# Choosing the unit blocks of a feed-forward layer: a multiply on GpSimd with a mask spread by DMA, in place of a third product on TensorE

## The chip, the cores and the metric

The kernel runs on one core of one Trainium2 chip. The metric is device time in microseconds of one execution. The time before is 1347.35 us, the median of three runs (1347.07 to 1347.78). Five engines work side by side, each with its own queue of instructions that it takes strictly in order: TensorE (PE in the profile; its weight loads are PEld), VectorE (DVE), ScalarE (ACT), GpSimd (POOL), and SyncE (SP), which here only issues DMAs.

## The reference

Two layers of a transformer block over x of shape 8 x 512 x 256. Layer 0 is an attention with 16 heads plus a mixture of 32 experts, layer 1 a small gelu layer plus a feed-forward layer whose units are chosen in blocks. Only the last one matters here:

```python
BLOCK, NBLK = 64, 16                  # 16 blocks of 64 hidden units
TOPK = NBLK // 4                      # a token keeps 4 of the 16 blocks
prob = softmax(xf @ router_w.T + router_b)
...
y = einsum('nib,dib->nd', where(mask[:, :, None], h, 0.0), w2b) + b2
```

Here h is relu(xf @ w1.T + b1), 1024 units to a token, and mask marks the 4 blocks with the largest prob. So a token's hidden units count only in the blocks that it chose.

## The kernel before

**An order made by a planner.** The kernel does not issue its work line by line. It first builds a list of operations (`op`, L156), each with an engine, a key, the function that issues its instructions, the operations it needs, a due time (`prio`), and the buffers that it takes (`acq`) and gives back (`rel`). `emit` (L206) then walks through a model of the five engines and picks, again and again, the operation that can start first; it issues the instructions in that order. The model's costs stand in the table `TIMES` (L52), the due times are shifted by the table `SHIFT` (L99), and `choose` (L295) prefers, on TensorE, an operation that keeps the tile layout of the one before (`SAME`, `OTHER`, L293). The layouts are F (the whole array), R (two halves of its rows), C (two halves of its columns), E and Q (quarters), G. Whatever the planner decides becomes the fixed order of every engine's queue; on the chip, semaphores only make an engine wait.

**The attention stage.** For 32 pairs of (batch, group of four heads), `produce` (L872) projects q, k, v, normalizes and transposes q and k; `attend` (L1133) then makes scores, an exponential, a division on GpSimd (`divide`, L1181), a transposition (`turn`, L1186; L419), its copies to SBUF into a buffer `prT` (L1199, L1201; two such buffers exist), and the product with v (`values`, L1222). The experts run in between. This stage fills the span up to about 1000 us.

**The second layer.** `second` (L1688) is called once for each of the eight batches b. With the lines that matter, in the order in which a batch goes through them:

- `s.root` (L1714, POOL): one over the root of the variance, 128x4. It comes after `s.eps` on DVE. `s.b2` (L1723, POOL, four to a batch) adds the output bias to the residual.
- `s.xn` (L1718, DVE, four) normalizes, `s.xT` (L1729, PE) transposes; the copies follow (L1735, L1737).
- `s.lg` (L1746, PE) makes the router's logits, `s.lgt` (L1768, PE) turns them; DVE and ACT make the softmax and mark the four largest (L1777 to L1792, `s.rep`).
- `s.off` (L1797, DVE) writes 1.0 for a block that is *not* chosen. `s.mt` (L1803, PE) turns these 128x128 tiles with four bf16 products, `s.mo` (L1810, ACT) copies them to SBUF as `offT`, a tile of 128 x 512 in which row k tells of block k.
- `s.narrow` and `s.gelu` (L1817, L1825): the small layer beside it.
- `s.hid` (L1844, PE), four times, two tiles of 128 units x 512 tokens each: two fp32 products for each tile (L1849), and a **third product** (L1853) of a constant table `blkm` with `offT`. `blkm` has -2^100 where a unit belongs to block k, so the sum becomes hugely negative for all units of the blocks that were left out.
- `s.relu` (L1865, ACT): relu with the bias. What was left out comes out as zero.
- `s.start` (L1888, PE) begins the output in PSUM with the small layer's part, `s.down` (L1896, PE), four to a batch, adds the product with w2; `s.out` (L1904, DVE) adds the residual, and a DMA on SP's queue writes 128 KB to the output (L1909).

The batches overlap: while batch b is in its `s.hid`, the four `s.down` of batch b-1 are put in between, and the front part of batch b+1. The tables `blkm` and the two buffers for `s.off` are made once by `c_masks` (L1514, key `w.masks`, POOL) in one of the five 4 KB buffers `ew`.

Of the kernel before, what the change touches and what calls it, by code (L numbers as in the profile page):

```python
# [11 lines left out]
ALU = mybir.AluOpType  # L12
# [33 lines left out]
class Op:  # L46
# [5 lines left out]
    "warm": (4137, 4117), "n.turn": (165, 317), "p1.qk": (2004, 1984), "p1.v": (891, 1041),  # L52
    "p.turn": (259, 412), "p2.qk.a": (1775, 1937), "p2.qk.b": (1730, 1932), "g.turn": (118, 282),
    "a.score2": (803, 976), "a.score0": (335, 497), "gt.turn": (328, 308), "a.score3": (1100, 1238),
    "p2.v.a": (897, 1041), "p2.v.b": (900, 1042), "a.turn2": (425, 586), "a.turn0": (140, 291),
    "a.score1": (541, 711), "a.turn3": (516, 662), "a.turn1": (289, 417), "a.y": (2305, 2374),
    "c.logits": (1854, 1924), "eb.turn": (608, 679), "c.turn": (605, 656), "c.merge": (1865, 1933),
    "c.mturn": (368, 439), "o.proj.a": (3468, 3674), "o.proj.b": (3500, 3628), "e.hidden": (1854, 1924),
    "e.turn": (493, 655), "e.down": (1865, 1934), "w.t1.t": (446, 600), "w.t3.t": (495, 565),
    "w.t4.t": (164, 328), "w.t2.t": (586, 650), "w.fold.t": (1035, 1106), "j.go": (1075, 1145),  # L60
    "s.xT0.t": (447, 600), "s.xT1.t": (437, 600), "s.lg": (574, 644), "s.lgt": (165, 327),
    "s.narrow": (949, 1084), "s.mt": (224, 387), "s.hid": (3873, 4029), "s.start": (532, 626),
    "s.down": (3471, 3617), "n.stat": (329, 408), "n.aggr": (76, 150), "gw.uk": (335, 417),
    "n.eps": (64, 156), "n.xv": (350, 410), "gw.sum": (328, 410), "n.out0": (200, 278),
    "gw.prod": (598, 686), "gw.max": (70, 308), "gw.red": (598, 676), "gw.inv": (85, 164),
    "gw.mul": (71, 150), "qw": (37, 116), "om1": (82, 157), "p.sum": (599, 682), "p.mean": (74, 168),
    "om3": (86, 172), "p.g": (75, 156), "p.scale": (663, 693), "p.gs": (72, 156), "p.k1": (261, 343),
    "p.k0": (261, 342), "om4": (184, 164), "om5": (195, 175), "g.least": (108, 196), "g.relu": (78, 168),
    "g.s0": (69, 166), "g.s1": (159, 252), "g.s2": (82, 176), "g.s3": (91, 176), "g.s4": (81, 174),
    "g.s5": (90, 175), "g.s6": (162, 192), "g.s7": (84, 174), "see": (15, 60), "g.s8": (90, 166),  # L70
    "g.s9": (89, 175), "g.s10": (91, 175), "g.s11": (84, 174), "g.s12": (74, 174), "g.s13": (104, 174),
    "g.out0": (333, 416), "a.most2": (475, 662), "a.most0": (208, 392), "a.inv": (79, 160),
    "a.most3": (606, 791), "a.out02": (467, 551), "gt.out": (121, 206), "a.out00": (198, 281),
    "a.most1": (340, 526), "a.out03": (601, 685), "n.shift": (70, 155), "a.out01": (326, 412),
    "c.max": (584, 676), "c.inv": (176, 156), "c.prob": (425, 494), "c.max8": (592, 676),
    "c.rest": (673, 678), "eb.out": (331, 416), "c.sel": (615, 682), "c.out": (604, 688),
    "c.mout": (364, 425), "c.min": (334, 416), "o.add": (337, 416), "e.hout": (599, 689),
    "e.bias": (603, 680), "e.out": (332, 418), "w.t1.o": (601, 682), "w.t3.o": (469, 449), "w.wide": (0, 0),
    "w.t4.o": (1207, 1187), "w.fold.o": (201, 284), "j.add": (600, 682), "s.tiles": (0, 0),
    "s.stat": (320, 408), "s.aggr": (84, 166), "s.eps": (100, 170), "s.xn": (394, 599),  # L80
    "s.xT0.o": (605, 691), "s.lgb": (267, 351), "s.most": (174, 219), "s.sub": (139, 224),
    "s.sum": (137, 220), "s.inv": (88, 178), "s.prob": (179, 226), "s.max8": (78, 159), "s.top": (150, 178),
    "s.rep": (143, 165), "s.off": (215, 195), "s.out": (340, 425), "gw.sq": (361, 418),
    "n.out1": (155, 270), "p.qk": (477, 586), "p.sq": (531, 633), "om2": (219, 199), "p.v": (259, 372),
    "p.q0": (252, 364), "p.q1": (255, 367), "biasrows": (733, 798), "g.exp": (117, 216),
    "g.out1": (257, 364), "a.exp2": (608, 809), "a.exp0": (400, 596), "a.out12": (363, 474),
    "a.exp3": (716, 917), "a.out10": (156, 266), "a.exp1": (501, 702), "a.out13": (467, 586),
    "n.xa": (497, 601), "a.out11": (330, 372), "a.yout": (473, 585), "c.bias": (585, 687),
    "c.exp": (723, 918), "e.gelu0": (536, 630), "e.gelu1": (521, 624), "w.t2.o": (473, 607),
    "s.xT1.o": (605, 585), "s.exp": (276, 256), "s.gelu": (403, 383), "s.mo": (471, 586),  # L90
    "s.relu": (707, 687), "masks": (855, 891), "rows": (2373, 2353), "slopes": (613, 593),
    "n.root1": (516, 556), "clear": (544, 524), "gw.root": (987, 1010), "p.root": (1622, 1643),
    "zeros": (251, 311), "g.off": (236, 216), "g.part": (305, 389), "g.rest": (409, 434), "begun": (0, 0),
    "a.div2": (569, 585), "a.div0": (347, 371), "a.div3": (667, 691), "n.root4": (985, 1013),
    "a.div1": (450, 478), "w.masks": (3007, 3024), "w.small": (166, 187), "w.fill": (537, 572),
    "s.root": (1037, 1017), "s.b2": (746, 768),
# [3 lines left out]
    "c.bias": -3.29, "s.max8": 3.57, "p.q0": 2.42, "w.t4.o": -5.8, "s.eps": -9.92, "c.max8": 2.15,  # L100
    "p2.v.a": -3.63, "s.mt": 5.88, "a.exp3": -4.3, "w.t4.t": -0.13, "o.proj.b": 0.15, "s.lgt": -7.35,
    "c.exp": 2.7, "p.sum": -5.14, "c.mout": 0.03, "s.b2": 7.43, "s.xT1.o": -4.3, "s.lgb": -4.56,
    "a.out10": 0.14, "a.exp1": -0.68, "a.yout": -3.47, "s.exp": -10.95, "a.most0": 0.35, "g.s3": 3.95,
    "s.narrow": -4.78, "s.root": -4.04, "s.sum": 1.37, "g.s6": 2.17, "s.most": -2.85, "s.stat": -0.87,
    "s.prob": -1.71, "p.sq": -1.43, "w.fold.o": 2.03, "p.gs": -2.82, "c.turn": 1.44, "g.s12": 1.31,
    "s.top": -6.26, "g.s10": -1.46, "g.s2": 3.5, "eb.turn": -2.98, "w.t1.o": -3.61, "om1": -7.04,
    "biasrows": 4.93, "a.div0": 6.33, "gw.root": -2.34, "gw.inv": -3.63, "s.gelu": -0.89, "a.out13": 1.66,
    "masks": -48.39, "s.start": 5.05, "g.s9": -2.47, "w.small": -3.28, "w.fill": 15.3, "s.xT0.o": -1.94,
    "n.root1": 1.13, "n.root4": 3.27, "g.least": 2.04, "e.out": -0.02, "gt.out": -2.41, "c.logits": -7.82,
    "s.off": 4.99, "clear": 3.53, "g.relu": 0.52, "warm": -21.2, "g.s0": -1.94, "a.turn3": 0.39,  # L110
    "a.score3": -1.07, "g.s4": -1.71, "s.inv": -4.39, "qw": -14.97, "g.s5": 5.68, "g.exp": -1.07,
    "om2": -5.05, "a.turn2": 1.14, "e.gelu0": 5.01, "p.q1": -5.55, "j.go": -3.38, "c.min": 8.72,
    "a.out00": 2.71, "e.turn": -1.46, "a.y": 1.34, "s.hid": -2.92, "s.sub": -9.5, "w.fold.t": -8.73,
    "p.qk": -0.3, "a.inv": -1.61, "gw.uk": -5.57, "c.out": 2.42, "n.shift": 7.81, "a.turn1": -0.19,
    "p.g": -3.58, "e.hidden": 0.67, "c.merge": 4.93, "a.div2": -2.99, "p.mean": -0.88, "slopes": -2.76,
    "a.div1": -2.14, "a.out12": 0.32, "g.out1": 0.43, "a.out02": 2.95, "e.gelu1": -0.41, "s.relu": -1.14,
    "o.add": -4.81, "n.turn": -1.67, "w.t2.o": 1.33, "a.most3": -3.64, "g.s11": -2.41, "s.out": 7.6,
    "n.xa": 7.52, "om4": 10.76, "w.t3.o": 1.73, "g.turn": -1.73, "g.s1": 5.26, "c.prob": 2.06,
    "c.rest": 3.9, "c.mturn": 9.1, "begun": 1.87, "gw.prod": 1.93, "rows": -0.26, "n.eps": -2.59,
    "j.add": -4.89, "e.hout": 1.27, "s.mo": -1.28, "n.aggr": -8.37, "c.inv": 5.78, "s.tiles": -5.37,  # L120
    "a.score0": -1.86, "s.xT1.t": -3.79, "gw.red": -4.57, "p2.v.b": -1.01, "e.bias": -0.22, "p.v": -5.67,
    "g.part": 0.41, "g.out0": 0.1, "p.k0": -1.07, "c.max": 5.04, "om5": 2.2, "s.xT0.t": -5.16,
    "o.proj.a": 1.19, "s.lg": -9.54, "a.out03": -2.66, "g.rest": 5.2, "eb.out": -6.2, "gt.turn": 6.11,
    "see": -4.13, "gw.sum": 2.3, "s.aggr": -12.41, "a.exp2": 1.42, "g.s7": 5.88, "p1.v": 5.24,
    "s.xn": -3.43, "w.t3.t": -3.47, "gw.max": -3.1, "g.off": 6, "p.scale": 3.47, "w.t1.t": -2.48,
    "w.t2.t": 0.97, "p2.qk.b": 0.14, "s.down": 7.43, "a.out01": -0.8, "a.exp0": 1.45, "g.s13": 1.57,
# [1836 lines left out]
```

## Time and profile before

| what | value |
|---|---|
| median of the runs | 1347.35 us |
| the profiled execution's own time | 1349.12 us |
| its span | 1347.4 us |
| TensorE busy in the span | 1302.8 us |
| the same, 50 to 1000 us | 925.13 of 950 us |
| the same, 1000 to 1100 us | 95.63 of 100 us |
| the same, 1100 to 1347.4 us | 243.69 of 247.4 us |
| GpSimd busy, 1100 to 1347.4 us | 22.18 of 247.4 us |
| third products (L1853) | 64, first at 1048.6 us, last at 1325.2 us |

The profile is of one execution, whose own time is 1.7 us above its span. Busy time of TensorE is modelled: matmuls are pipelined, a matmul's listed duration reaches into the next one's, so what one costs is read from the distance between starts. In a timeline row the columns are: start, busy time of the merged row, engine, line, operation, out<-in, tile of the array, shape, count, and in brackets the idle time before it and who ended it.

### The profile page before, as it was taken

To read this page: it belongs to the slowest core of one execution; us is meant where nothing else is said; L and a number is where in the kernel's file an instruction comes from. 1 tells how busy PE (TensorE), PEld (TensorE's weight loads), DVE (VectorE), ACT (ScalarE), POOL (GpSimd) and SP (SyncE) were. 2 spreads that over 40 slices of the span, in tenths; PEclk is the share of its full clock that TensorE was granted. 3 is DMA by queue.
4 is the path that set the end of the run, shared out by engine and by line. 5 is a ranking of instruction groups with operands and counts; after the bars stand their busy time and mean duration, and the time that the engine had idled before them with its cause. 6 is when DMAs were issued, how large, how long until landed. Compare 5 with 4: busy or idle time off the path is not lost.

```text
span 1347.4 us, 32371 instructions
## 1 busy us (share of the span) xinstructions
PE 1302.8 (97%) x11831; PEld 829.9 (62%) x11840; DVE 901.1 (67%) x3712; ACT 820.6 (61%) x2268; POOL 621.4 (46%) x1115
## 2 busy tenths in 40 slices
PE   7899999999999999999999999999999999999998
PEld 4555666556655665665565656656665576666666
DVE  5889987787777778867877677778869433232300
ACT  3687876676677757766866766777757522222221
POOL 4666644656456555645565455555545311111100
PEclk8899999999999999999999999999999999999999
DMA  7002001431143032322323231142120000000000
GB/s 225 5 1 80 2 2 63 143 127 67 64 145 118 12 127 84 117 78 81 125 69 126 80 132 64 64 147 67 56 71 17 1 13 13 16 17 16 16 20 20
DMA packets 74575, 90.65 MB, mean 67 GB/s; under 512 B 5272, under 2 KB 57744, under 8 KB 74416
## 3 DMA queue, kind: packets, MB, share of 16 engines
q1 hardware_dynamic: 73856, 88.16, 19.5%
q8 instruction: 93, 1.52, 0.5%
q14 instruction: 66, 0.54, 0.1%
q10 hardware_dynamic: 560, 0.43, 0.1%
HBM read 84.11 MB, written 4.19 MB: 66 GB/s over the span
## 4 chain that ended last, share of the span: by engine, by line
PE 69%; DVE 19%; ACT 5%; POOL 4%; issue 2%; DMA 1%; SPq 0%; DVEq 0%; ACTq 0%; POOLq 0%
PE w L440 25%; PE w L1896 8%; PE w L1849 8%; PE w L1155 7%; PE w L1227 6%; PE w L419 5%; DVE pr L1164 5%; DVE prT L1201 3%; POOL rs L964 2%; DVE ss L957 2%; DVE tm L967 2%; PE w L1151 2%; PE w L1337 1%; DVE k L991 1%; ACT pr L1172 1%
## 5 line engine op out<-in xcount | busy, mean ns | idle before, releaser
L1182 POOL TENSOR_SCALAR pr<-pr,rinv 128x384 f32<-128x384 f32 (+3 forms) x512 | 284.6, 573 | 241.9 <-DVE rinv L1179 177.4
L1172 ACT ACTIVATE pr<-pr,nm 128x384 f32<-128x384 f32 (+3 forms) x512 | 285.6, 563 | 47.6 <-DVE nm L1164 38.8
L964 POOL TENSOR_TENSOR rs<-ss,nhalf 128x8 f32<-128x8 f32 x128 | 213.6, 1671 | 152.4 <-DVE ss L960 139.6
L1164 DVE CUSTOM_DVE_ANT_0 pr<-w,later 128x384 f32<-128x384 f32 (+3 forms) x512 | 241.3, 485 | 49.3 <-PE w L1155 47.0
L440 PE MATMUL w<-wqk_sb,xnT 64*128 64x512 f32 x992 | 243.4, 605 | 0.8 <-DVE ms L817 0.2
L1155 PE MATMUL w<-k,q 64*128 64x128 f32 (+3 forms) x1024 | 189.3, 442 | 0.0
L1227 PE MATMUL w<-prT,v 128*64 128x512 f32 (+3 forms) x1024 | 154.1, 443 | 9.4 <-DVE prT L1201 5.0
L1199 ACT COPY prT<-w 128x512 f32<-128x512 f32 (+3 forms) x256 | 106.5, 430 | 84.0 <-PE w L419 83.4
L419 PEld LDWEIGHTS w<-ident,pr 64*128 64x128 f32 x2560 | 115.5, 139 | 64.7 <-issue 38.7
L440 PEld LDWEIGHTS w<-wqk_sb,xnT 64*128 64x128 f32 x992 | 93.3, 188 | 69.1 <-issue 61.1
L1227 PEld LDWEIGHTS w<-prT,v 128*64 128x64 f32 x1024 | 72.1, 138 | 101.5 <-issue 62.6
L1201 DVE COPY prT<-w 128x512 f32<-128x512 f32 (+3 forms) x256 | 122.8, 485 | 11.2 <-PE w L419 9.7
L440 PE MATMUL w<-wvg_sb,xnT 64*128 64x260 f32 x992 | 126.5, 388 | 0.0
L419 PE MATMUL w<-ident,pr 64*128 64x64 f32 x2560 | 120.9, 223 | 5.2 <-DVE k L991 1.9
L1849 PE MATMUL w<-xT,mT 128*128 128x512 f32 x256 | 120.6, 593 | 0.5
L440 PE MATMUL w<-wp_sb,yT 64*128 64x256 f32 x1024 | 117.1, 379 | 1.0 <-DVE seen L451 0.7
L1904 DVE TENSOR_TENSOR ot<-w,x 128x256 f32<-128x256 f32 x32 | 13.5, 423 | 149.1 <-PE w L1896 149.1
L440 PEld LDWEIGHTS w<-wp_sb,yT 64*128 64x128 f32 x1024 | 99.4, 187 | 17.0 <-issue 3.4
L1155 PEld LDWEIGHTS w<-k,q 64*128 64x128 f32 x1024 | 89.3, 189 | 21.4 <-issue 17.5
L938 ACT COPY tm<-w 128x512 f32<-128x512 f32 x128 | 72.9, 588 | 47.8 <-PE w L440 29.2
L957 DVE TENSOR_REDUCE ss<-sq 128x8 f32<-128x512 f32 x128 | 87.2, 681 | 22.1 <-ACT sq L942 22.1
L967 DVE TENSOR_TENSOR tm<-tm,rs 128x512 f32<-128x512 f32 x128 | 90.7, 710 | 13.2 <-POOL rs L964 12.7
(210 smaller groups left out, 2025.0 us busy)
## 6 DMA issues: line engine op xcount, KB each, us to landing
ew<-in_L_ffn_w_dram SPq DMA_DIRECT2D x128, 512.0 KB
x<-in_L_attn_x_dram SPq DMA_DIRECT2D x15, 512.0 KB
out_dram<-ot SPq DMA_DIRECT2D x32, 128.0 KB
raw<-in_L_ffn_w_dram SPq DMA_DIRECT2D x4, 512.0 KB
wqk_sb<-in_L_attn_Wk_dram SPq DMA_DIRECT2D x4, 256.0 KB
wqk_sb<-in_L_attn_Wq_dram SPq DMA_DIRECT2D x4, 256.0 KB
wp_sb<-in_L_attn_Wproj_dram SPq DMA_DIRECT2D x1, 1024.0 KB
b2g<-in_L_ffn_w_dram SPq DMA_DIRECT2D x32, 32.0 KB
```

The source lines that it names most:

```text
L419: nc.tensor.transpose(out, blk, ident[rows, rows])
L440: x = nc.tensor.matmul(m.outs[i], lhs(i, k, rows), rhs(k, rows), start=(part == k == 0), stop=(part == 1 and k == n - 1))
L957: nc.vector.tensor_reduce(s.ss[t], s.sq[t], AX.X, ALU.add)
L964: nc.gpsimd.tensor_tensor(s.rs[t], s.ss[t], nhalf[:, : 2 * HG], ALU.pow)
L967: nc.vector.tensor_mul(s.tm[t], s.tm[t], s.rs[t].unsqueeze(2).to_broadcast([P, 2 * HG, D]),)
L1155: nc.tensor.matmul(m.sc[h][:, :w], s.qT[k, q, n0:w], s.kT[k, q, :w], start=False, stop=True)
L1164: nc.vector.tensor_tensor_reduce(m.p[:, h, :], m.sc[h][:, :w], later[:, T - w :], -1.0, BIG, ALU.add, ALU.min, m.nm[:, h : h + 1],)
L1172: nc.scalar.activation(m.p[:, h, :], m.p[:, h, :], AF.Exp, bias=m.nm[:, h : h + 1], scale=-1.0, accum_out=m.sums[:, h : h + 1],)
L1182: nc.gpsimd.tensor_scalar(m.p[:, h, :], m.p[:, h, :], m.rinv[:, h : h + 1], 1.0, ALU.mult, ALU.mult)
L1201: nc.vector.tensor_copy(dst, src)
L1227: nc.tensor.matmul(pp.yp[h * D : (h + 1) * D, j * P :], s.v[j][:, hh * D : (hh + 1) * D], pp.tri[:, :, h, j : j + 4 * (NT - 1 - j) + 1 : 4 ...
L1849: nc.tensor.matmul(m.ph[i], w1T[:, dc, k * P : (k + 1) * P], s.xT[:, dc, :], start=(dc == 0), stop=False,)
```

## The change

The mask is now applied after the relu, by a multiply. `s.off` writes 1.0 for a *chosen* block, in fp32, into the place of the probabilities. `s.mt` turns 128 x 16 to 16 x 128 four times in fp32. `s.mo` copies 16 rows. Then a DMA sends these 16 rows of 512 tokens (bf16) to a scratch tile in DRAM, and two DMAs read it back so that each of the 128 partitions gets the row of its own block, for all eight tiles: a mask of 128 x 8 x 512 bf16, 1 MB. It lies in one of the two buffers `prT`, which the attention has used. Third products, `blkm` and `c_masks` go. GpSimd multiplies each rectified tile by its mask in place (`s.keep`, 128x512, 64 in all), and `s.start` waits in the plan for the multiplies instead of the relus. `s.hid` no longer needs the mask.

The rest is the planner's: all numbers of `TIMES` and `SHIFT` are others, and so are `SAME` and `OTHER`. The order of the whole kernel is made anew from them, in the attention stage too.

```diff
-    "c.bias": -3.29, "s.max8": 3.57, "p.q0": 2.42, "w.t4.o": -5.8, "s.eps": -9.92, "c.max8": 2.15,
+    "c.bias": -4.03, "s.max8": -0.29, "p.q0": -5.16, "w.t4.o": -4.68, "s.eps": -8.83, "c.max8": 2.96,
...
-    SAME, OTHER = 0.8, 0.8
+    SAME, OTHER = 1.6, 1.2
...
+    dram = ctx.enter_context(tc.tile_pool(name="dram", bufs=1, space=bass.MemoryType.DRAM))
...
-        c_mk = op("POOL", "w.masks", c_masks, (), at + 2.0, acq=["ew"])
...
-            def left_out():
-                s.off = cw.off[plan.now.got["off"][0]]
-                nc.vector.tensor_scalar(s.off[:, :, :NBLK], s.rp[:, :, :NBLK], 0.0, None, ALU.is_ge)
+            def chosen():
+                s.kept = s.pp[:, :, :NBLK]
+                nc.vector.tensor_scalar(s.kept, s.rp[:, :, :NBLK], 0.0, None, ALU.is_lt)
...
             def turn5(pt):
                 for t in range(NT):
-                    nc.tensor.matmul(
-                        pt[:, t * P : (t + 1) * P], s.off[:, t, :], ident16,
-                        start=True, stop=True,
-                    )
+                    nc.tensor.transpose(pt[:NBLK, t * P : (t + 1) * P], s.kept[:, t, :], ident)
...
+            def m_send():
+                s.rows = dram.tile([NBLK, T], BF16, tag=f"kept{b}", name=f"kept_{b}")
+                nc.sync.dma_start(s.rows, s.keptT[:NBLK])
+
+            def m_spread():
+                s.mask = held("prT", [P, NFC, T], f"mask_{b}", dtype=BF16)
+                for h in range(2):
+                    nc.sync.dma_start(
+                        s.mask[h * BLK : (h + 1) * BLK],
+                        s.rows.rearrange("(k h) t -> h k t", h=2)[h].unsqueeze(0).to_broadcast(
+                            [BLK, NFC, T]),
+                    )
...
-            a = op("PE", "s.mt", m_go, [off], w + 2.5, acq=["b"], rel=[(off, "off", 0)])
+            a = op("PE", "s.mt", m_go, [off], w + 2.5, acq=["b"], rel=[f"pp{b % 2}"], mode="E")
             mk = op("ACT", "s.mo", lambda: out5(boxm[0]), [a], w + 2.6, acq=["v"], rel=[(a, "b", 0)])
+            sent = op("DMA", 100, m_send, [mk], w + 2.7, rel=[(mk, "v", 0)], lat=2000)
+            mk = op("DMA", 3400, m_spread, [sent], w + 2.8, acq=["prT"], lat=2000)
...
-                                start=(dc == 0), stop=False,
+                                start=(dc == 0), stop=(dc == NC - 1),
                             )
-                        nc.tensor.matmul(
-                            m.ph[i],
-                            cw.blkm[:, 2 * k : 2 * k + 2, :].rearrange("p a f -> p (a f)"),
-                            s.offT, start=False, stop=True,
-                        )
...
+                def choose(i, kp=kp):
+                    k = 2 * kp + i
+                    nc.gpsimd.tensor_tensor(s.hT[k], s.hT[k], s.mask[:, k, :], ALU.mult)
+
-                a = op("PE", "s.hid", hidden, xT + w_1 + [mk, pa], w + 3.5 + 0.8 * kp,
-                       acq=["w", "hold"], rel=last)
+                a = op("PE", "s.hid", hidden, xT + w_1 + [pa], w + 3.5 + 0.8 * kp,
+                       acq=["w", "hold"], rel=mine)
...
+                    kept.append(op("POOL", "s.keep", lambda i=i, f=choose: f(i), [hid[-1], mk],
+                                   w + 3.9 + 0.8 * kp + 0.1 * i, rel=[(mk, "prT", 0, NFC)]))
...
-                go = op("PE", "s.start", start, [gl, w_a, *hid], w + 7.0 + 1.8 * t, acq=["w"],
+                go = op("PE", "s.start", start, [gl, w_a, *kept], w + 7.0 + 1.8 * t, acq=["w"],
```

## The prediction

> **What bounds the kernel now.** First the head of the page, then its slices, to see which engine is full and where.
>
> ```profile
> span 1347.4 us, 32371 instructions
> ...
> PE 1302.8 (97%) x11831; PEld 829.9 (62%) x11840; DVE 901.1 (67%) x3712; ACT 820.6 (61%) x2268; POOL 621.4 (46%) x1115
> ...
> PE   7899999999999999999999999999999999999998
> ...
> POOL 4666644656456555645565455555545311111100
> PEclk8899999999999999999999999999999999999999
> ```
>
> TensorE is full in every slice but the first, and GpSimd nearly idle in the last nine, where the changed work lies. Next the busy time of stretches of that end: stretch, PE, PEld, DVE, ACT, POOL, granted clock, DMA share, GB/s.
>
> ```profile
> 1100.00:1150.00 50.00, 49.89 (x263) 33.03 (x263) 21.19 (x78) 10.46 (x16) 5.84 (x8) 1.00 0.04 14
> 1150.00:1200.00 50.00, 49.95 (x217) 30.99 (x220) 12.02 (x43) 15.21 (x23) 5.82 (x8) 1.00 0.04 14
> 1200.00:1250.00 50.00, 49.89 (x235) 33.63 (x230) 14.49 (x70) 14.01 (x21) 4.68 (x6) 1.00 0.06 20
> ```
>
> TensorE rests 0.05 to 0.11 us in 50, at full clock, so a product taken away there shortens the end by what it takes, as long as no new wait appears. Because busy is modelled, I take the price from distances between starts, in TensorE's timeline.
>
> ```profile
> 1264.67 1.04 PE L1729 MATMUL w<-ident,xn 128*128 128x128 f32 x8
> 1265.63 1.13 PE L1888 MATMUL w<-cw,cgT 64*128 64x256 f32 x8
> ...
> 1286.82 1.88 PE L1849 MATMUL w<-xT,mT 128*128 128x512 f32 x4
> 1288.54 0.38 PE L1853 MATMUL w<-offT,cm 128*128 128x512 bf16 x1
> 1288.76 1.88 PE L1849 MATMUL w<-xT,mT 128*128 128x512 f32 x4
> ...
> 1306.18 0.39 PE L1803 MATMUL w<-ident,cm 128*128 128x128 bf16 x4
> 1306.40 3.67 PE L1896 MATMUL w<-w2T,wqk_sb 128*128 128x256 f32 x16
> ```
>
> The fp32 part of a hidden tile occupies 1288.54 - 1286.82 = 1.72 us, the third product 0.22 us, not the 0.38 us listed.
>
> **The change, part by part.**
>
> *Removed on TensorE:* 64 third products x 0.22 = 14.1 us, one after the other on the path (53 rows of them wake ACT's relu).
>
> *Made dearer on TensorE:* `s.mt`. Four bf16 products took 0.22 us (1306.18 to 1306.40). The four new ones also run over 128 columns, in fp32. The nearest row is L1729: 8 fp32 transposes from 1264.67 to 1265.63, 0.12 us each, so 0.48. The ends are 0.22 (as before) and 4 x 0.16 = 0.64, since the single L1768 starts 0.16 us ahead of its successor. I take 0.48: 8 x 0.26 = 2.1 us lost.
>
> *Added on GpSimd:* 64 multiplies of 128x512. The trace has no such row. Its two-operand multiplies and adds are 217 ns for 128x16 (L1066) and 730 ns for 128x256 (L1723): 2.14 ns for each further element of a row, so 730 + 256 x 2.14 = 1.28 us. Ends: 0.73 (no dearer than half the size) and 1.46 (twice it). Eight make 10.2 us for a batch, beside 4 x 0.70 us for `s.b2` and 1.02 for `s.root` (L1714); a batch takes about 33 us of TensorE, so GpSimd has the time. [...]
>
> *Added DMAs and the wait behind them.* This is what can spoil the gain, since GpSimd takes its queue in order. In the listed order of the changed kernel the queue is: eight `s.keep` of batch b, four `s.b2` of b, `s.root` of b+2, then `s.keep` of b+1. So a late mask delays not only its own multiplies but the norm of b+2, which TensorE needs for `s.xT` of b+2. TensorE's order from the end of `s.mt` of b to that `s.xT` is: three pairs of hidden tiles (6 x 1.72 = 10.3), one `s.down` (3.5), `s.lgt` (0.16), two `s.down` (7.0), `s.start` (1.07), `s.narrow` (1.0), one pair of hidden tiles (3.44): a cover of 26.5 us. The first `s.down` of b itself comes 1 us later still.
>
> Against it stands: ACT's copy (0.2 + 0.59); the store of 16 rows and the load of 1 MB, neither in the trace. For the store, the last output store ended the span 2.7 us after its VectorE add (1344.67 to 1347.4). For the load, the 512 KB of L1254, alone on the queues:
>
> ```profile
> 1027.21 0.39 SPq L1254 DMA_DIRECT2D x<-in_L_attn_x_dram  x1
> ...
> 1028.00:1029.00 1.00, 1.00 (x10) 0.63 (x7) 1.00 (x4) 1.00 (x3) 0.00 (x0) 1.00 0.41 52
> 1029.00:1030.00 1.00, 1.00 (x17) 0.81 (x17) 1.00 (x4) 0.93 (x4) 0.00 (x0) 1.00 0.92 326
> 1030.00:1031.00 1.00, 1.00 (x10) 0.43 (x8) 1.00 (x5) 1.00 (x4) 0.41 (x1) 1.00 0.48 163
> ```
>
> It is over 3.8 us after its issue, and moves 326 GB/s once it runs; another 512 KB add 1.6 us. The mask is there at 0.8 + 2.7 + 3.8 + 1.6 = 8.9 us. Then 10.2 (multiplies) + 2.8 (`s.b2`) + 1.0 (`s.root`) + 1.5 for four `s.xn` (0.35 each when GpSimd rests, L1718, plus a hop) = 24.4 us, 2.1 us ahead of TensorE. So I cost it at nothing, hidden by the `s.down` of the batch before. The low end for the load is that of 512 KB (mask at 7.3). The high end is the rate of a load that reads the same rows for many partitions, L1285's 128 KB at 72 GB/s in 304 to 305 us: 14.6 us for 1 MB, mask at 19, TensorE waits 8 us. I take the value by L1254 because L1285's four loads of 32 KB are issued 0.45 us apart, which alone makes 72 GB/s. [...]
>
> The end: `s.mt` of the last batch comes ahead of all its hidden tiles; 8 x 1.72 + two `s.down` + `s.start` + two more = 28.9 us lie before its first `s.down`, more than 8.9 + 10.2. After it nothing changes: 14.1 us of `s.down`, an add, a store.
>
> *The seam to the attention, 1000 to 1100 us.* Before, TensorE lost time there: 0.18, 1.89 and 0.78 us idle from 1036 to 1042, and a clock of 0.57 from 1040 to 1048, in which a product with v took 4.5 us instead of 2.3. About 5 us in all, with `s.mt` of batch 0 close behind the softmax. After, hidden tiles need no mask and fill the seam. But the eight multiplies of batch 0 stand in GpSimd's queue ahead of the last two divisions of the attention: from `s.mt` of batch 0, these are done at 8.9 + 10.2 + 1.0 = 20.1 us, and TensorE wants them at about 20.5. Gain 0 to 5, loss 0 to 3 with the mask at 12.
>
> *The new order of the attention.* The TensorE instructions of this stage are the same, and changes of tile layout number 282 in the new order against 278. What can differ is the idle time, 25 us from 50 to 1000 us. In the listed order I summed TensorE's work between dependent steps. Last transposition to the product with v, under 1 us: 13 pairs of 64 against 8. Projection to its transposition, under 5 us: 7 against 4. Waits of these two kinds cost 0.7 us (5.0 us in 7, L1227 for `prT`) and 0.4 us (1.9 us in 5, L419 for `tm`): 5 x 0.7 + 3 x 0.4 = 5 us lost. Most of the new short gaps lie in the first five groups, where VectorE is the fuller engine (46.8 us busy in 100 to 150), so it may be less; at most the idle time doubles, 25 us, at least half of it goes, 12. I set the seam's gain against this loss.
>
> *At nothing:* `c_masks` (3 us of GpSimd at 954 us, ahead of need); `s.off` and `s.mo`, the same shape in time or less.
>
> **Sum.** 14.1 - 2.1 = 12.0 us, the rest at zero: 1349.12 - 12.0 = 1337.1 us for an execution like the profiled one. This one was 1.8 us above the median, so for the median 1335 us.
>
> **Rivals.**
> - *The mask comes late (slower).* Place: GpSimd's queue, in which the roots of batches 2 to 7 stand behind the multiplies of 0 to 5. From a mask at 8.9 + 2.1 = 11.0 us on, each further microsecond costs six. At 13.0 us the gain is gone, at 15 us the time is 1347 - 12 + 24 = 1359; with L1285's rate 1347 - 12 + 48 = 1383. For it speaks that every DMA but 1 MB of them is known and that a read of so few rows is not; against it the 326 GB/s.
> - *The multiply is slow.* It needs over (10.2 + 2.1) / 8 = 1.54 us; at 1.8 us the stall is 2.1 x 6 = 12 us and the time that of before, 1348. The high end of the rows, 1.46, is below it.
> - *The new order loses more.* 12 us of new waits in the attention: about 1347.
> - *The new order gains,* 12 us and the seam's 5: about 1320.
> - That the third products stay or the multiplies land elsewhere is excluded: the listing has 64 products less, 64 multiplies on GpSimd.
>
> **Chances.** What a measurement here can tell from no change is about 0.2%, 2.7 us. Forecast (1329 to 1341) 0.60; order gains more 0.07; order loses (1341 to 1352) 0.15; mask late 0.13; multiply slow 0.05. Of the losing order 0.06 are still faster and 0.06 the same; of the late mask 0.04 and 0.02; of the slow multiply 0.01 and 0.02. So faster 0.78, same 0.10, slower 0.12. The range goes from 1325, with half of the order's gain, to 1350, and leaves out some 0.15.
>
> **What would show it.** Right: stretches at the end still with TensorE idle below 0.2 us in 50, batches 1.5 us shorter, multiplies of about 1.28 us, the mask's landing to the first multiply below 9 us after `s.mt`. Wrong: L1717 (`s.xT`) waiting for VectorE's `xn` behind GpSimd's root, once in every batch; the first `s.down` of a batch waiting for GpSimd; or over 30 us idle from 50 to 1000 us.

## The result

| | before | after |
|---|---|---|
| median time | 1347.21 us (4 runs, 1346.33 to 1347.78) | 1368.31 us (4 runs, 1364.16 to 1369.54) |
| ratio | | 1.0152, 95% interval 1.0129 to 1.0175 |
| span of the profiled execution | 1347.4 us | 1367.4 us |
| its mean granted clock | 0.992 | 0.988 |
| TensorE idle, 50 to 1000 us | 24.9 us | 35.3 us |
| TensorE idle, 1000 to 1100 us | 4.4 us | 3.8 us |

The change makes the kernel 1.5% slower. The forecast was 1335 us with a range of 1325 to 1350: wrong in sign and size.

### The profile after

The head of the page and two of its slice rows, for the kernel after:

```profile
span 1367.4 us, 32288 instructions
...
PE 1310.2 (96%) x11776; PEld 836.9 (61%) x11776; DVE 920.8 (67%) x3712; ACT 821.5 (60%) x2269; POOL 678.0 (50%) x1177
...
PE   7799999999999999999999999999999999999999
...
PEclk9999999999999999999999999999999999999999
```

TensorE is as full as before, but busy for 7.4 us longer (1310.2 - 1302.8), with 64 products fewer to do. So the head does not say where the time went. The busy time of stretches (columns as in the prediction: the granted clock is the third number from the right) shows the end of the kernel:

```profile
1150.00:1200.00 50.00, 50.00 (x216) 31.87 (x215) 16.20 (x74) 16.45 (x24) 20.36 (x21) 1.00 0.15 35
...
1300.00:1350.00 50.00, 50.00 (x193) 32.91 (x192) 6.08 (x25) 13.14 (x19) 23.37 (x24) 1.00 0.27 59
```

In these stretches TensorE now rests not at all, and the norm's transpositions `s.xT` (L1717, L1729 before) return every 31.92 us, as two of these rows show:

```profile
1196.67 1.04 PE L1717 MATMUL w<-ident,xn 128*128 128x128 f32 x8
...
1228.59 1.04 PE L1717 MATMUL w<-ident,xn 128*128 128x128 f32 x8
```

Before, they came at uneven distances, two batches apart 1235.85 - 1168.97 = 66.88 us, 33.44 each. The batch is 1.52 us shorter, and the end is what was forecast. The loss lies ahead of it: the last product with v starts at 1118.2 us, not 1087.2.

The rows of the matmuls, from which the prediction took its waits, show only a part of what moved there: TensorE's idle time from 50 to 1000 us grew by 10.4 us (24.9 to 35.3). More of it stands in the rows of the weight loads. Their waits, 50 to 950 us, before: engine, line waited at, who ended it, us in total, times, longest.

```profile
PEld w L419 <- POOL pr L1182: 5.9, 19, 0.8
PEld w L419 <- DVE tm L967: 5.7, 16, 0.9
PEld L421 <- POOL gtm L1077: 5.2, 10, 1.0
```

The same view after:

```profile
PEld w L420 <- POOL pr L1183: 24.4, 68, 1.1
...
PEld w L420 <- DVE tm L968: 16.3, 28, 1.8
PEld L422 <- POOL gtm L1078: 16.0, 22, 1.3
```

Three results of other engines came late by 16.8 us in all before, by 56.7 us after: the softmax's divided scores (GpSimd's L1183, 68 times), the scaled projection `tm` (VectorE), and the bf16 copies `gtm` (GpSimd). For the first it is the number of waits that grew, 19 to 68, at 0.31 us each before and 0.36 after. The same three lead the matmuls' own list after (8.9 us for `tm`, 6.5 for `gtm`, 5.8 for the divided scores). Not all waits grew: those of the weight loads for any result of another engine went from 90.9 to 116.2 us, 25.3 more, since the others fell by 14.6. Weight loads overlap matmuls (836.9 us of the ones beside 1310.2 of the others in a span of 1367.4), so part of such a wait is covered by the matmuls still running, and what is not covered shows only in part as idle time ahead of the next matmul (116.2 us of these waits from 50 to 950 us, 35.3 us of idle time from 50 to 1000). That a queue is taken strictly in order, as the section on the chip has it, therefore does not mean for TensorE that one instruction ends before the next begins.

**Theory:** the mechanism (mask and multiplies) gains its 12 us, and the attention order that the planner made from the new numbers loses by such waits what is missing, some 33 us (the 21.1 by which the median rose and the 12 that the mechanism gains). **Rival:** the mechanism itself costs the time, by the mask's DMAs, by GpSimd's queue, or at the seam.

### The profile page after: what moved, and what is told of

Read it like the earlier page. It is cut to its first block, busy times and chain, and to the rows that moved or that the text cites. A ratio compares the mean times of both kernels' runs of the same rounds, so it can differ in the third digit from the quotient of the medians.

```text
span 1367.4 us, 32288 instructions
## 1 busy us (share of the span) xinstructions
PE 1310.2 (96%) x11776; PEld 836.9 (61%) x11776; DVE 920.8 (67%) x3712; ACT 821.5 (60%) x2269; POOL 678.0 (50%) x1177
## 3 DMA queue, kind: packets, MB, share of 16 engines
q8 instruction: 93, 1.52, 0.5%
## 4 chain that ended last, share of the span: by engine, by line
PE 56%; DVE 21%; ACT 10%; POOL 7%; issue 4%; DMA 2%; SPq 0%; ACTq 0%; DVEq 0%; POOLq 0%
PE w L441 19%; PE w L1896 8%; PE w L1849 8%; PE w L1156 5%; PE w L420 5%; PE w L1228 4%; DVE pr L1165 4%; ACT pr L1173 3%; DVE gp L570 3%; POOL rs L965 2%; DVE ss L958 2%; DVE k L992 2%; DVE prT L1202 2%; POOL pr L1183 2%; POOL gtm L1078 1%
## 5 line engine op out<-in xcount | busy, mean ns | idle before, releaser
L1183 POOL TENSOR_SCALAR pr<-pr,rinv 128x128 f32<-128x128 f32 (+3 forms) x512 | 274.9, 553 | 371.8 <-DVE rinv L1180 275.5
L1173 ACT ACTIVATE pr<-pr,nm 128x128 f32<-128x128 f32 (+3 forms) x512 | 285.0, 559 | 64.5 <-DVE nm L1165 57.9
L1165 DVE CUSTOM_DVE_ANT_0 pr<-w,later 128x128 f32<-128x128 f32 (+3 forms) x512 | 235.6, 483 | 35.6 <-PE w L1156 33.8
L441 PE MATMUL w<-wqk_sb,xnT 64*128 64x512 f32 x992 | 249.4, 619 | 2.0 <-DVE seen L452 2.0
L1156 PE MATMUL w<-k,q 64*128 64x128 f32 (+3 forms) x1024 | 182.9, 438 | 0.0
L441 PEld LDWEIGHTS w<-wqk_sb,xnT 64*128 64x128 f32 x992 | 100.4, 194 | 71.6 <-issue 63.1
L986 ACT ACTIVATE q<-w,w 128x128 f32<-128x128 f32 x256 | 89.4, 366 | 82.5 <-PE w L420 65.7
L441 PE MATMUL w<-wvg_sb,xnT 64*128 64x260 f32 x992 | 135.7, 389 | 1.6 <-DVE seen L452 1.3
L1200 ACT COPY prT<-w 128x384 f32<-128x384 f32 (+3 forms) x256 | 102.6, 423 | 40.8 <-PE w L420 39.0
L1904 DVE TENSOR_TENSOR ot<-w,x 128x256 f32<-128x256 f32 x32 | 13.6, 425 | 153.7 <-PE w L1896 152.5
L1849 PE MATMUL w<-xT,mT 128*128 128x512 f32 x256 | 113.9, 596 | 0.1
```

The source lines that it names most:

```text
L441: x = nc.tensor.matmul(m.outs[i], lhs(i, k, rows), rhs(k, rows), start=(part == k == 0), stop=(part == 1 and k == n - 1))
L1156: nc.tensor.matmul(m.sc[h][:, :w], s.qT[k, q, n0:w], s.kT[k, q, :w], start=False, stop=True)
L1165: nc.vector.tensor_tensor_reduce(m.p[:, h, :], m.sc[h][:, :w], later[:, T - w :], -1.0, BIG, ALU.add, ALU.min, m.nm[:, h : h + 1],)
L1173: nc.scalar.activation(m.p[:, h, :], m.p[:, h, :], AF.Exp, bias=m.nm[:, h : h + 1], scale=-1.0, accum_out=m.sums[:, h : h + 1],)
L1183: nc.gpsimd.tensor_scalar(m.p[:, h, :], m.p[:, h, :], m.rinv[:, h : h + 1], 1.0, ALU.mult, ALU.mult)
L1849: nc.tensor.matmul(m.ph[i], w1T[:, dc, k * P : (k + 1) * P], s.xT[:, dc, :], start=(dc == 0), stop=(dc == NC - 1),)
```

## The experiments

All times are medians, with ratios to runs of the kernel before on the same chip.

| kernel | us | ratio, 95% interval | product with v of pair 54 starts at |
|---|---|---|---|
| before | 1347 | 1 | 926.4 |
| new_mech_old_order | 1345.39 | 0.9982 (0.9973 to 0.9992) | 923.3 |
| new_mech_old_order_fit | 1332.50 | 0.9891 (0.9873 to 0.9909) | 927.6 |
| old_no_third | 1333.51 | 0.9892 (0.9874 to 0.9909) | 925.4 |
| after | 1368.31 | 1.0152 (1.0129 to 1.0175) | 962.6 |
| old_mech_new_order | 1389.16 | 1.0306 (1.0283 to 1.0330) | 954.9 |
| after_mask_two_hops | 1383.42 | 1.0264 (1.0243 to 1.0284) | 962.0 |

The last column is a mark near the end of the attention. The first four kernels have TensorE's old order up to there, the last three the new one: 923 to 928 us against 955 to 963, whichever mechanism the last stage uses. TensorE has run 9162 or 9163 matmuls by then in the old order and 9198 or 9199 in the new, so the work ahead of the mark is nearly the same. That puts the loss on the order. (That old_mech_new_order is 7.7 us ahead of the changed kernel there is by an estimate mostly the clock, see the last section.)

### Mechanism and order, exchanged

The new mechanism in the old attention order: `TIMES` and `SHIFT` of the changed kernel for the keys that begin with s., w. or j., of the kernel before for all others.

```diff
-    "c.bias": -4.03, "s.max8": -0.29, "p.q0": -5.16, ...
+    "c.bias": -3.29, "s.max8": -0.29, "p.q0": 2.42, ...
-    SAME, OTHER = 1.6, 1.2
+    SAME, OTHER = 0.8, 0.8
```

> The mask and the multiplies on GpSimd as in the changed kernel, but the attention in the order of the kernel before: the planner gets its old durations, shifts and preferences for every operation of the attention, and the new ones only for those of the last stage (s., w., j.). TensorE's order is then that of before up to some 950 us. Theory (the mechanism gains some 12 us in the last stage, the new attention order loses some 33 us): 1347 - 12 = 1335 us, 1328 to 1342. Rival (the mechanism itself, its DMAs and its place in GpSimd's queue, costs the time): about that of the changed kernel, 1360 to 1370 us.

Measured: 1345.39 us. Neither number. The attention is as fast as before (923.3 us in the table), but the end did not follow. The stretches of this kernel show it:

```profile
980.00:990.00 10.00, 6.22 (x71) 4.44 (x73) 9.09 (x32) 4.33 (x15) 2.90 (x5) 0.96 0.06 14
990.00:1000.00 10.00, 10.00 (x80) 4.86 (x80) 5.63 (x16) 4.71 (x13) 2.58 (x4) 0.87 0.01 2
```

TensorE waits 3.8 us between 980 and 990 us, and the clock dips behind that. The last stage's shifts had been made to meet another attention order. So a second cost had to be told apart, that of the mismatch at the seam.

The old mechanism in the new attention order, by the reverse edit on the kernel before (all of `TIMES` and `SHIFT` is the changed kernel's, but for the hidden tile's duration):

```diff
-    "c.bias": -3.29, "s.max8": 3.57, "p.q0": 2.42, ...
+    "c.bias": -4.03, "s.max8": -0.29, "p.q0": -5.16, ...
-    SAME, OTHER = 0.8, 0.8
+    SAME, OTHER = 1.6, 1.2
```

> The third product as in the kernel before, but the attention in the order of the changed kernel: its durations, shifts and preferences for the planner, with the hidden tile's old duration. TensorE's order is that of the changed kernel up to some 970 us. Theory (order): 1347 + 33 = 1380 us, 1372 to 1386. Rival (mechanism): about that of the kernel before, 1342 to 1352 us.

Measured: 1389.16 us, 3 us above the theory's range and far from the rival's. The waits of its weight loads are those of the changed kernel, without any of its mechanism:

```profile
PEld w L419 <- POOL pr L1182: 23.4, 66, 1.1
...
PEld w L419 <- DVE tm L967: 17.3, 31, 1.8
```

The waits for `gtm` are 15.3 us. The seam costs again, here between 1040 and 1080 us (TensorE busy 7.64, 9.12, 7.65 and 7.29 of 10 us in four stretches, 8.3 us idle), about the excess over 1380, though the execution profiled was the quickest of four, 1384.74 us.

### Which of the planner's numbers

Two kernels put back one part of the changed kernel's numbers each: new_only_pref the two preferences, new_only_shift the old `SHIFT` for all keys but s., w. and j.

```diff
-    SAME, OTHER = 1.6, 1.2
+    SAME, OTHER = 0.8, 0.8
```

```diff
-    "c.bias": -4.03, ... "p.q0": -5.16, ...
+    "c.bias": -3.29, ... "p.q0": 2.42, ...
```

> The changed kernel with the planner's two preferences (SAME, OTHER) put back from 1.6 and 1.2 to 0.8 and 0.8; durations and shifts stay new. If the two preferences make the bad order, 1335 to 1345 us; if the shifts or durations do, 1360 to 1375 us. By the mechanism rival 1365 to 1370 us whatever the order.

> The changed kernel with the old shifts for the operations of the attention; its new durations and preferences stay. If the shifts make the bad order, 1335 to 1345 us; if the preferences or durations do, 1360 to 1375 us. By the mechanism rival 1365 to 1370 us whatever the order.

Measured: 1395.42 us (ratio 1.0354, 1.0334 to 1.0375) and 1384.92 us (1.0277, 1.0256 to 1.0297). Both miss every expectation. The numbers are one fitted set: taking back a part makes a third order, worse than both. No single one of them can be blamed.

### The mechanism in an order that fits it

As new_mech_old_order, with the last stage's shifts (s., w., j.) fitted to the old attention order and the stage begun 0.6 earlier:

```diff
-    "w.t2.t": 1.81, ... "s.xT0.o": -2.97, ... "s.down": 8.73, ...
+    "w.t2.t": -1.17, ... "s.xT0.o": -4.08, ... "s.down": 9.31, ...
-            second(b, NIT * NU - 9.0 + CU * b)
+            second(b, NIT * NU - 9.6 + CU * b)
```

> As new_mech_old_order, which lost some 9 us between 980 and 1090 us because shifts of the last stage made for one attention order met another; here only the shifts of the last stage's operations (s., w., j.) and the start of that stage (9.0 to 9.6) are fitted anew, by the planner's own plan, whose end comes 13 us ahead of that of the kernel before. The same fitting of the kernel before moved its plan by 0.05 us, so what it gains is not the fitting's own. TensorE's order is that of before up to some 950 us. Theory (mechanism 12 us better, order all of the loss): 1335 us, 1331 to 1340. Rival (the mask and the multiplies cost at the seam whatever the order): 1342 to 1348.

Measured: 1332.50 us, 14.3 us ahead of the kernel before, and the best version of this study. Its waits are those of before:

```profile
PEld w L420 <- POOL pr L1183: 6.3, 20, 0.8
PEld w L420 <- DVE tm L968: 5.5, 16, 0.9
```

The removed step alone, in the kernel before with every order unchanged (the choice of blocks is left out):

```diff
-                                start=(dc == 0), stop=False,
+                                start=(dc == 0), stop=(dc == NC - 1),
...
-                        nc.tensor.matmul(
-                            m.ph[i],
-                            cw.blkm[:, 2 * k : 2 * k + 2, :].rearrange("p a f -> p (a f)"),
-                            s.offT, start=False, stop=True,
-                        )
```

> The kernel before, its order on every engine and its tables unchanged, without the 64 third products: the choice of blocks is left out. This prices the removed step alone. Theory (0.22 us each, one after the other on TensorE's path): 1347 - 14 = 1333 us, 1331 to 1336. Rival (part of it was hidden behind something else): 1338 us or more.

Measured: 1333.51 us, 13.3 us ahead. Two of its batches take 63.42 us (1226.48 - 1163.06), 31.71 each: 1.73 below before, 8 x 0.216 us.

### How late the mask may be

Two more copies of the kept rows, DRAM to DRAM, ahead of the mask's load, in the changed kernel:

```diff
                 s.mask = held("prT", [P, NFC, T], f"mask_{b}", dtype=BF16)
+                for n in range(2):
+                    rows = dram.tile([NBLK, T], BF16, tag=f"hop{n}_{b}", name=f"hop{n}_{b}")
+                    nc.sync.dma_start(rows, s.rows)
+                    s.rows = rows
```

> The changed kernel, same order, with two more copies of the kept rows from DRAM to DRAM between their store and the mask's load, so that each mask comes later by two round trips, some 2 x 2.5 = 5 us. The prediction gave 2.1 us of slack in GpSimd's queue and six microseconds for each one beyond: (5 - 2.1) x 6 = 17 us slower, 1380 to 1392. With the slack that the trace of the changed kernel suggests (the last product of batch 2 in GpSimd ends 1.3 us ahead of the next root) it is the same or more. Rival (the wait is hidden more deeply, by other work that may go ahead): 1364 to 1372.

Measured: 1383.42 us, 15.1 us slower than the changed kernel and within the range expected by the prediction's account. Transpositions of this kernel in the last stage, and GpSimd's multiplies of batch 2:

```profile
1173.96 0.61 PE L1791 MATMUL w<-ident,cw 128*16 128x128 f32 x4
...
1202.83 1.74 PE L1717 MATMUL w<-ident,xn 128*128 128x128 f32 x8 [1.78 <-DVE xn L1706]
...
1239.22 1.73 PE L1717 MATMUL w<-ident,xn 128*128 128x128 f32 x8 [1.93 <-DVE xn L1706]
...
1272.46 1.74 PE L1717 MATMUL w<-ident,xn 128*128 128x128 f32 x8 [0.46 <-DVE xn L1706]
```

```profile
1189.68 8.95 POOL L1870 TENSOR_TENSOR wqk_sb<-wqk_sb,mask 128x512 f32<-128x512 f32 x8 [22.79 <-DMA mask<-hop]
```

The first multiply starts 1189.68 - 1173.96 = 15.7 us after `s.mt`, against 1180.84 - 1169.74 = 11.1 in the changed kernel. The mask is 4.6 us later and TensorE waits 1.78 us at the next but one norm: the slack of its first transposition was 2.8 us. The row of eight takes 1.74 us, not 1.04, so the slack of the last was about 2.1 us, as forecast for all four `s.xn`. The queue of GpSimd does what the prediction feared: the root of batch 4 starts 1201.31 - 1173.96 = 27.4 us after `s.mt`, with no idle time behind the multiplies and `s.b2`, against 1193.81 - 1169.74 = 24.1 in the changed kernel. But it does so over four batches, not six: four distances between `s.xT` from 1168.96 to 1305.84 add up to 136.9 us against 127.7, 9.2 us lost, among them 1.7 us by an `s.down` that took 5.31 us (at 1204.40) instead of 3.62, which the author put down to a dip of the clock. The rest is at the seam, where a division of the attention stands behind the multiplies of batch 0 (TensorE waits 2.8 us for it).

### The multiply on VectorE

In new_mech_old_order_fit (the planner's duration of the multiply changes too):

```diff
-                    nc.gpsimd.tensor_tensor(s.hT[k], s.hT[k], s.mask[:, k, :], ALU.mult)
+                    nc.vector.tensor_tensor(s.hT[k], s.hT[k], s.mask[:, k, :], ALU.mult)
...
-                    kept.append(op("POOL", "s.keep", lambda i=i, f=choose: f(i), [hid[-1], mk],
+                    kept.append(op("DVE", "s.keep", lambda i=i, f=choose: f(i), [hid[-1], mk],
```

> As new_mech_old_order_fit, with the 64 multiplies on VectorE, and their duration for the planner 0.6 instead of 1.23 us. If GpSimd is the right place because it rests, and its queue costs nothing: the same within 3 us. If waits behind the multiplies on GpSimd cost TensorE time: 3 to 8 us faster. If VectorE's other work (softmax of the router, additions, norm) is delayed: slower.

Measured: 1333.60 us (0.9893, 0.9878 to 0.9907), the same as on GpSimd. Groups of this kernel and of the changed one (busy us, mean ns):

```profile
L1866 DVE TENSOR_TENSOR wqk_sb<-wqk_sb,mask 128x512 f32<-128x512 f32 x32 | 20.8, 697 | 20.8 <-DMA mask<-kept 20.6
```

```profile
L1866 POOL TENSOR_TENSOR hT<-hT,mask 128x512 f32<-128x512 f32 x32 | 36.1, 1159 | 78.9 <-DMA mask<-kept 63.7 <-ACT hT L1860 15.1
```

VectorE needs 0.70 us for what takes GpSimd 1.16. It saves nothing, which fits a GpSimd whose queue costs TensorE nothing here.

### What the new order waits for

GpSimd's divisions, shortened to one column, in both orders (this leaves the scores undivided):

```diff
-                    m.p[:, h, :], m.p[:, h, :], m.rinv[:, h : h + 1], 1.0, ALU.mult, ALU.mult
+                    m.p[:, h, :1], m.p[:, h, :1], m.rinv[:, h : h + 1], 1.0, ALU.mult, ALU.mult
```

> The changed kernel, same order on every engine, with GpSimd's softmax divisions (L1183) shortened to one column of each half: they leave the scores undivided, and take some 0.1 us instead of 0.38 to 0.73. In the rows of TensorE's weight loads, waits for three results grew from the kernel before to the changed one (50 to 950 us): for GpSimd's divided scores from 5.9 to 24.4 us, for VectorE's scaled projection tm from 5.7 to 16.3, for GpSimd's bf16 copies gtm from 5.2 to 16.0; 40 us in all. Theory (these waits are what the new order costs): the 24 us go, and part of the waits for gtm, which stand in the same queue: 22 to 36 us faster, 1332 to 1346. Rival (the waits are a sign only, something else is due at the same moments, such as ACT's exponentials): under 10 us, 1358 or more.

> The control: the same shortening of the divisions in the kernel before, same order. Theory: its waits for the divided scores are 5.9 us and those for gtm 5.2, so 5 to 11 us faster, 1336 to 1342. Rival (divisions cost the same in any order): as much faster as the changed kernel.

Measured: 1341.31 us (0.9951, 0.9922 to 0.9981) and 1337.76 us (0.9922, 0.9893 to 0.9950). Both times are within the theory's ranges: the new order gains 27.0 us, the old one 9.6, so 17.4 us of its loss hang on the divisions. Waits of weight loads in after_short_div:

```profile
PEld w L420 <- DVE tm L968: 17.8, 30, 1.8
...
PEld L422 <- POOL gtm L1078: 8.7, 14, 0.8
...
PEld w L420 <- POOL pr L1183: 2.3, 6, 0.7
```

Those for the divided scores are nearly gone, those for `gtm`, from the same queue, halved; those for `tm` stay.

GpSimd's roots of the projections' norms, replaced by copies (the root is left out):

```diff
-                    nc.gpsimd.tensor_tensor(s.rs[t], s.ss[t], nhalf[:, : 2 * HG], ALU.pow)
+                    nc.gpsimd.tensor_copy(s.rs[t], s.ss[t])
```

> The changed kernel, same order, with GpSimd's roots of the projections' norms (L965, 1.65 us each, 128 of them) replaced by copies of some 0.25 us, which leaves the root out. They stand in the chain to tm and in the queue of the divisions. Theory: the 16.3 us of waits for tm go, and most of those for the divided scores and gtm that come of a full queue: 20 to 45 us faster, 1323 to 1348. Rival: under 10 us, 1358 or more.

> The control: the same copies in place of the roots in the kernel before, same order. Theory: of 5.7 us for tm, 5.9 and 5.2 for the divided scores and gtm most go: 6 to 15 us faster, 1332 to 1341. Rival: as much faster as the changed kernel.

Measured: 1354.72 us (1.0051, 1.0040 to 1.0062) and 1338.27 us (0.9925, 0.9897 to 0.9954). The new order gains 13.6 us, less than expected, the old one 9.1. Waits for `tm` fell only from 16.3 to 14.1 us, for the divided scores from 24.4 to 17.3: the root's 1.65 us are not what makes them late. A miss.

VectorE's scaling of the projections, which ends the chain to `tm`, shortened to one column of each head (the others stay unscaled), alone and with the divisions:

```diff
-                        s.tm[t], s.tm[t],
-                        s.rs[t].unsqueeze(2).to_broadcast([P, 2 * HG, D]),
+                        s.tm[t][:, :, :1], s.tm[t][:, :, :1], s.rs[t].unsqueeze(2),
```

> The changed kernel, same order, with VectorE's scaling of the projections (L968, 0.69 us each, 128 of them) shortened to the first column of each head, which leaves the other columns unscaled. It ends the chain to tm. Theory (the waits for tm, 16.3 us from 50 to 950, are the rest of what the new order costs): 13 to 24 us faster, 1344 to 1355. Rival (they are due at the same moment as something else, or the rest is clock and layout): under 6 us, 1362 or more.

> The control in the kernel before, whose waits for tm are 5.7 us. Theory: 3 to 9 us faster, 1338 to 1344. Rival: as much as the changed kernel.

> The changed kernel, same order, with both the divisions and the scaling shortened. Theory (waits for these two are the loss): some 15 us below after_short_div's 1341, 1322 to 1331, that is 5 to 13 us ahead of before_short_both. Rival (clock, layout or interleaving): 1335 or more, level with before_short_both or behind it.

> The control: both shortened in the kernel before. Theory: 2 to 5 us below before_short_div's 1338, 1332 to 1336.

Measured for the scaling: 1344.36 us (0.9984, 0.9970 to 0.9997) and 1337.12 us (0.9919, 0.9890 to 0.9948), 24.0 and 10.1 us less, so 13.9 us hang on it. The waits for `tm` of the new order fall to a third (16.3 us before), those for the divided scores stay, in after_short_scale:

```profile
PEld w L420 <- POOL pr L1182: 24.4, 70, 1.1
...
PEld w L420 <- DVE tm L968: 5.2, 9, 1.3
```

For both: 1329.76 us (0.9864, 0.9818 to 0.9910) and 1329.03 us (0.9859, 0.9830 to 0.9887), 38.6 and 18.2 us less. Both times in the new order were within their ranges, and the controls came 1 and 3 us below theirs. That both shortened kernels are level, where the new order was expected 5 to 13 us ahead, is a miss: in this the rival (clock, layout or interleaving) was right. The clock holds part of it. Each was run twice: after_short_both took 1332.27 us at a clock of 0.987 and 1327.24 at 0.992, before_short_both 1328.17 at 0.996 and 1329.88 at 0.995. By (1 - clock) x span the profiled execution of the one lost 17.3 us of clock and that of the other 5.3. But some 9 us of this difference lie in the first 50 us (a clock of 0.79 against 0.97), and the second executions differ by only 4 us of clock (10.6 against 6.6).

So, of the 35.8 us between the changed kernel and new_mech_old_order_fit, 20.4 (38.6 - 18.2) go when these two results come early. The clock is not a separate part beside them. Summed over stretches of 10 us from 50 to 1150 us, it cost an estimated 12.0 us in the changed kernel and 6.3 in after_short_both, against 3.4 in the kernel before and in before_short_both, and 1.7 in new_mech_old_order_fit; so nearly 6 of the 20.4 are dips that went with the waits. The remaining 15 us are open. The dips that stay are one part, an estimated 4.6 us (6.3 - 1.7). The waits of weight loads are not another as a whole: for all results of other engines they are 70.5 us in after_short_both and 73.3 in before_short_both. Of single waits those for `gtm` are a candidate that was not tried by itself.

## Why the prediction was wrong

Step by step, as it was set out:

- *Removed on TensorE,* 14.1 us: right. old_no_third measured 13.3, and 1.73 us in a batch.
- *`s.mt` dearer,* 2.1 us: right. A batch with the new mechanism takes 31.92 us (32.02 in new_mech_old_order_fit), without any choice 31.71, so 0.21 to 0.31 us a batch, 1.7 to 2.5 in all.
- *Added on GpSimd,* 1.28 us for a multiply: 1.16 for one alone, 1.12 each in a row of eight. The ends held it. The straight line through 128x16 and 128x256 was some 10% too dear.
- *Mask there 8.9 us after the end of `s.mt`:* 10.7 measured (in batch 2 `s.mt` starts at 1169.74 and takes 0.45 us, the first multiply starts at 1180.84), between the value taken and the dear end (written as 19, though its terms 0.8 + 2.7 + 14.6 give 18.1). These rows of the changed kernel give the parts, SP's queue and then GpSimd's:

```profile
1170.99 0.95 SPq L1799 DMA_DIRECT2D kept<-keptT  x1
1173.10 1.26 SPq L1804 DMA_DIRECT2D mask<-kept  x2
```

```profile
1180.84 8.95 POOL L1866 TENSOR_TENSOR wqk_sb<-wqk_sb,mask 128x512 f32<-128x512 f32 x8 [18.16 <-DMA mask<-kept]
...
1193.81 1.01 POOL L1702 TENSOR_TENSOR rs_c<-ve_c,nhalf 128x4 f32<-128x4 f32 x1 [1.28 <-DVE ve_c L1700]
```

The store is issued 0.8 us after the end of `s.mt`, as forecast, the load 2.1 us later (2.7 forecast), and the first multiply starts 7.7 us later still (5.4 forecast). The load is the term that was mis-sized. Stretches of 1 us of the changed kernel, the last column GB/s:

```profile
1174.00:1175.00 1.00, 1.00 (x4) 0.47 (x3) 0.00 (x0) 0.57 (x1) 0.00 (x0) 1.00 0.37 122
1175.00:1176.00 1.00, 1.00 (x4) 0.48 (x3) 0.00 (x0) 0.40 (x1) 0.00 (x0) 1.00 1.07 256
...
1178.00:1179.00 1.00, 1.00 (x4) 0.49 (x3) 0.00 (x0) 0.00 (x0) 0.00 (x0) 1.00 1.15 191
```

It moved some 190 to 256 GB/s, not the 326 of L1254. Whether that is because the same rows are read for many partitions was not tried. The cheaper multiplies gave 1.2 of the 1.8 us back (9.0 instead of 10.2), and the root of batch 4 (the second row of GpSimd) waited for VectorE's `ve_c`, not for the queue. *Hidden, at nothing:* right, with 2.1 to 2.8 us to spare by the two hops.
- *The seam,* gain of 0 to 5: right in sign. Idle time from 1000 to 1100 us fell by 0.6 us, and the dip of the clock from 1040 to 1048 us, (1 - 0.57) x 8 = 3.4 us before, is gone.
- *The new order of the attention,* 5 us lost and set against the seam's gain: **this is the step that failed.** It lost some 36 us (1368.31 - 1332.50, the changed kernel against the same mechanism in a fitted old order). It listed two kinds of distance, last transposition to the product with v and projection to its transposition, and counted five and three short ones more, at 0.7 and 0.4 us. The first kind did not lose: the product with v waited 5.0 us for VectorE's `prT` before, and after no such wait is left from 50 to 1000 us. The second was counted too low: 1.2 us were planned, and 13.9 hang on the scaling that ends it. The costliest kind was not listed: from the scores through exponential and GpSimd's division to the transposition of the scores, 24.4 us of waits, 17.4 us by the shortened divisions. (The two do not add up, both together gave 20.4.) And idle time in front of matmuls, from which the prices came, shows only a part: it grew by 10.4 us (24.9 to 35.3), under a third of the loss. The bound that the text called the most, a doubling of the 25 us of idle time, was thus no bound. Nor was VectorE the fuller engine from 100 to 150 us, which was to soften the loss: it was busy 46.8 us there, TensorE 47.3.
- *Sum:* -12.0 from the terms that were worked out. new_mech_old_order_fit measured -14.3, with an order of its own at the seam.

Of the rivals the mask and the multiply were judged rightly. "The new order loses more" was the right rival with a wrong size, 12 us for 36. The sign that the text named for a wrong forecast, over 30 us idle from 50 to 1000 us, came true (35.3). The sign that the mask comes within 9 us failed (10.7) and did no harm, by the slack that remained.

## What to carry to other kernels

Where a planner makes the order, a change of its numbers is a change of the whole kernel: price the order that comes out of it, in every stage, as carefully as the edit itself, or test the edit in the old order. Read waits where they stand, in the rows of the weight loads as well as in those of the matmuls; idle time in front of matmuls was under a third of what an order cost here. And numbers fitted for one order are worth little in another: new_mech_old_order lost 12.9 us until its last stage was fitted.

## What the runs showed of the hardware

TensorE's granted clock fell to 0.50 for a few microseconds behind short idle times: in the changed kernel at some 92 to 99, 140 to 143, 164 to 167, 270 to 273 and 430 to 437 us. By stretches of 10 us, whose clock is then 0.83 or 0.66 (0.98 and 0.84 where a fall lies across two of them), that took some 1.7 or 3.4 us each time. The changed kernel, stretches of 2 us:

```profile
88.00:90.00 2.00, 1.34 (x20) 0.91 (x15) 2.00 (x11) 2.00 (x9) 0.95 (x2) 1.00 0.01 4
90.00:92.00 2.00, 1.16 (x17) 0.82 (x17) 2.00 (x7) 1.88 (x8) 2.00 (x3) 1.00 0.00 0
92.00:94.00 2.00, 1.43 (x18) 1.11 (x20) 2.00 (x8) 1.39 (x5) 1.32 (x3) 0.55 0.04 8
94.00:96.00 2.00, 2.00 (x20) 1.40 (x18) 1.71 (x7) 1.75 (x6) 0.41 (x1) 0.50 0.02 4
```

From 88 to 92 us TensorE idled 0.66 + 0.84 = 1.50 us, in pieces none of which was above 0.81 us. Then the clock fell: it was 0.60 in the stretch from 92 to 93 us, 0.50 from there until 99, and 1.00 again from 100. (The 0.57 us idle from 92 to 94 came mostly with the fall or behind it.) The changed kernel has five such places from 50 to 500 us, where the kernel before has none (1.00 in every stretch of 10 us); so here the order with more short waits paid for some of them twice. It did not pay alike in every execution: of the changed kernel's four, three had a mean clock of 0.988 and took 1367.45 to 1369.54 us, one had 0.991 and took 1364.16. For old_mech_new_order, with the same attention order, the author's estimate is 3.4 us lost by the clock from 50 us to the mark of pair 54, at one place (90 to 100 us), and for the changed kernel 12.0, which would be most of the 7.7 us between them there. What sets such a fall off is not shown. Ahead of the one above stood pieces of 0.81 and 0.64 us within four. The sum of idle time is not enough: at 58.7 us the kernel before had idled 2.58 us in one piece, and its clock stayed at 1.00.
